# Pinning the involution's products in VectorE's order while keys and values are made

## The chip, the cores and the metric

The kernel runs on one core of one Trainium2 chip. The metric is device microseconds from the start to the end of one execution. All data are float32. The engines named below are PE (TensorE, with PEld for its weight loads), DVE (VectorE), ACT (ScalarE), POOL (GpSimd) and SP (SyncE, which only issues transfers here).

## The reference, cut to what matters

The input x has 4 images of 512 channels and 64 x 64 pixels. Layer 0 is self-attention over the 4096 pixels of an image with 128 inner channels. Layer 1 is a bottleneck block whose middle is an involution: a 7 x 7 convolution whose weights are made from the data, pixel by pixel.

```python
# layer 0, n = 4096 pixels of one image
q, k, v = wq @ x + bq, wk @ x + bk, wv @ x + bv            # 128 x n each
attn = softmax(q.T @ k, axis=-1)
x = wo @ (v @ attn.T) + bo + x                             # 512 x n
# layer 1
o1 = relu(s1 * (W1 @ x) + b1)                              # 128 x n
w = Ws @ relu(sr * (Wr @ o1) + br) + bs                    # 49 taps for each of 8 groups, per pixel
inv[c, pixel] = sum over 49 taps of w[group of c, tap, pixel] * o1[c, pixel moved by the tap]
out = s3 * (W3 @ inv) + b3 + x
```

## The kernel before, in words

**Stages.** The images b = 0 to 3 run one after the other. For each, `keys_values(b)` makes keys and values of 8 chunks of 512 pixels: four `pk` products (512 columns) and 16 `pv` products (128 columns) for each chunk. Then `attention(b)` goes through 8 blocks of 512 queries with 32 steps each: scores `pss` on PE, exponential `pt` on ACT, the product `po` with the values on PE, and the running sum `pacc` of the exponentials on DVE. After the last image a tail finishes what is left.

**Work woven in.** All that follows attention is cut into generators that are advanced by `chores()`, which is called four times for each chunk of `keys_values` and once for each step of `attention`. Three lists hold them:

- `finishing` (`finish_block`): what follows a block of queries. The row sums are inverted (`pl`, `rls`, `spread`), four `pwo` products are made, each of which DVE adds to x (L515), then the product `p1`, ACT's relu `o1` (L528), DVE's transpose `o1t` (L559), whose result eight transfers on SP write to `pix` in DRAM (L569), and `pr` and `red`, from which the tap weights come.
- `units`, worked off by `involution()` (L291 and on): a unit is four image rows. Its tap weights `pw` come from one step on PE. Then there are 14 (or 21) products: DVE multiplies image rows in a ring buffer by tap weights (L341), at first into `acc` and then into one of four `prod` buffers, and POOL adds each `prod` to `acc` (L365). Two last additions on POOL (L376) fold `acc`. The ring is loaded from `pix` by SP (`pump()`, L247). A product is called below by its place in its unit; product 0 is the one into `acc`.
- `closing` (`turn_unit`, `close_chunk`): transposes `pa` of a unit's `acc` on PE, ACT's copy to `accT` (L404), and, when two units make a chunk, four `py` products with W3, each of which DVE scales and adds to x (L419); then the store.

While keys and values of image b are made, the last pieces of image b-1 run beside them: the block finished last (chunk 7), chunk 5's `py`, the last products of unit 11, all of unit 12 and the first of unit 13. Image 0's stage has no earlier image beside it.

**PSUM.** `pl`, `spread`, `pwo`, `p1`, `pa`, `py`, `pr` and `pq` share the two buffers of the tag `mm`: a product into one of them waits for the reader of what was there before. `pw` has one buffer.

**What sets the order.** The Python code gives instructions in program order, with a model of the time of each engine: `pe` counts the time of PE's products, and `free` tells how long DVE, POOL and the DMA engines are booked. `involution()` gives no product while POOL is booked for longer than `lag` beyond `pe`. `lag` is `POOL_LAG[0]`, 4.0 us, in `keys_values`, and `POOL_LAG[1]`, 7.5 us, in `attention` and the tail:

```python
    for b in range(B):
        lag = POOL_LAG[0]
        kv = keys_values(b)
        lag = POOL_LAG[1]
```

The compiler then builds an instruction list for each engine. It follows program order as a priority, but by its own reckoning of times it takes an instruction that is ready before one that is not. So the order on an engine can differ from the program's. `tc.keep_in_program_order(ins)` gives the compiler an edge from the last instruction that the program gave to the same engine to `ins`: `ins` is not issued ahead of that one. It adds no wait at run time. The kernel before uses it in two other places (L282, L664).

Of the kernel before, what the change touches and what calls it, by code (L numbers as in the profile page):

```python
# [72 lines left out]
POOL_LAG = 4.0, 7.5  # L73
# [8 lines left out]
def fast_path(  # L82
# [20 lines left out]
    nc = tc.nc  # L103
# [51 lines left out]
    lag = 0.0  # L155
    low, load = 0, 0

    def until(us):
        while pe < us and not tail:
            yield "wait"  # L160
# [5 lines left out]
    def takes(engine, us):  # L166
        free[engine] = max(free[engine], pe) + us
        return free[engine]
# [39 lines left out]
    def mm(o, lhsT, rhs, start=True, stop=True, shared=1):  # L208
        pe_us(rhs.free_size() * PE_COLUMN / shared)
        return nc.tensor.matmul(o, lhsT=lhsT, rhs=rhs, start=start, stop=stop)  # L210
# [19 lines left out]
    def pump():  # L230

        nonlocal load
        while load // STEP in written:
            b, row = divmod(load, STEP)
            rows, us = written[b]

            end = H + SR - UR if rows == H else rows + PAD - 1
            n = min(b * STEP + end, low + RING) - load
            n = min(n, RING - load % RING, PIECE if b == B - 1 else RING)
            if n <= 0:  # L240
                break
            for h in range(2):
                src = pix[b % 2][row + h : row + h + n, :W, :]
                windows = bass.AP(
                    tensor=src.tensor, offset=src.offset, ap=[[P, W], [WP * P, n], [1, K * P]]
                )
                nc.sync.dma_start(  # L247
                    ring[h * W : (h + 1) * W, load % RING : load % RING + n]
                    .rearrange("p r x c -> p r (x c)"),
                    windows,  # L250
                )
            free["dma"] = max(free["dma"], us)
            us = takes("dma", ROW_US * n) + LAND_US
            landing.update((load + i, us) for i in range(n))
            load += n
            if row + n == H + SR - UR:
                load = (b + 1) * STEP
# [7 lines left out]
    def weights(b, u):  # L265
        red, col = reds[b, u]
        wpools.append(wpools.pop(0))
        pw = wpools[0].tile([P, NT, CH], F32, tag="w", name=f"pw_{b}_{u}")
        for t in range(NT):

            rows = slice(t * (P // NT), t * (P // NT) + CR + 1)
            pixels = slice(col, col + P)
            mm(
                pw[:, t, : NTAP * G], red[rows, pixels], wt[rows, O_WT : O_WT + NTAP * G],
                shared=2,
            )
        return pw


    def judge():  # L280
        ok = const.tile([P, B * N // TB], F32, name="ok")
        tc.keep_in_program_order(nc.vector.tensor_scalar(ok, rls, SAFE[0], None, ALU.is_ge))  # L282
        nc.vector.scalar_tensor_tensor(ok, rls, SAFE[1], ok, ALU.is_le, ALU.mult)
        okr = const.tile([P, 1], F32, name="okr")
        nc.vector.tensor_reduce(okr, ok, AX.X, ALU.min)
        pn = ps.tile([1, 1], F32, tag="mm", name="pn")
        nc.tensor.matmul(pn, lhsT=okr, rhs=ones[:, :1], start=True, stop=True)
        nc.vector.tensor_scalar(verdict, pn, P - 0.5, None, ALU.is_lt)


    def involution():  # L291
        nonlocal low, due
        while True:
            while not units:
                yield "none"
            b, u = units.pop(0)
            acc = work2.tile([P, NT, 4, P], F32, tag="acc", name=f"acc_{b}_{u}")
            yield from until(free["dve"] + 0.3)
            pw = early.pop((b, u), None) or weights(b, u)
            begin = pe + 0.5  # L300
            accp, ops = None, []
            base = b * STEP + u * UR
            for dy0, n in DYS:

                at = (base + dy0) % RING
                whole = at + n + NT < RING + 1
                pieces = [(dy0, n)] if whole else [(dy0, 2), (dy0 + 2, n - 2)]
                ops += [(x, dy, k) for x in range(K) for dy, k in pieces]
            for o, (x, dy, n) in enumerate(ops):
                if o and dy >= DYS[1][0] > ops[o - 1][1]:  # L310
                    low = base + UR
                    pump()
                    if tail and units:
                        early[units[0]] = weights(*units[0])
                rows = [(base + dy + t * 2) % RING for t in range(NT)]
                while base + dy + n + NT > load:
                    yield "wait"
                landed = max(landing[base + dy + i] for i in range(n + NT))
                while not tail and (
                    pe < max(begin, landed)  # L320
                    or free["dve"] > pe + (4.5 if b == B - 1 else 3.5)
                    or free["pool"] > pe + lag
                ):
                    yield "wait"
                free["pool"] = max(free["pool"], takes("dve", DVE_TAPS[0] + DVE_TAPS[1] * n))
                takes("pool", POOL_TAPS[0] + POOL_TAPS[1] * n)
                due -= n
                d0 = dy - DYS[dy >= DYS[1][0]][0]
                first = x == 0 and dy < DYS[1][0]
                prod, p0 = acc, d0  # L330
                if not first:
                    prod, p0 = prods.tile(
                        [P, NT, 4, P], F32, tag="prod", name=f"prod_{b}_{u}_{o}"
                    ), 0
                col = (x * K + dy) * G
                lines = ring[:, rows[0] : rows[0] + n, x, :]
                image = bass.AP(
                    tensor=lines.tensor, offset=lines.offset,
                    ap=[lines.ap[0], [(rows[1] - rows[0]) * K * P, NT], [K * P, n], [1, P]],
                )  # L340
                nc.vector.tensor_tensor(  # L341
                    prod[:, :, p0 : p0 + n, :].rearrange("p t d (g c) -> p t d g c", g=G),
                    image.rearrange("p t d (g c) -> p t d g c", g=G),
                    pw[:, :, col : col + n * G].unsqueeze(3)
                    .broadcast_to([P, NT, n * G, GC])
                    .rearrange("p t (d g) c -> p t d g c", d=n),
                    ALU.mult,
                )
                if first:
                    pass  # L350
                elif tail and o % 2 and (accp is not None or n > 1):

                    begin_sum = accp is None
                    if begin_sum:
                        accp = ps1.tile(
                            [P, NT, 2, P], F32, tag=("po", "acc")[u % 2], name=f"accp_{b}_{u}"
                        )
                    for d in range(0, n, 2):
                        k = min(2, n - d)
                        mm(  # L360
                            accp[:, :, :k, :], ident, prod[:, :, d : d + k, :],
                            begin_sum and d == 0, o + 2 >= len(ops) and d + 2 >= n,
                        )
                else:
                    nc.gpsimd.tensor_tensor(  # L365
                        acc[:, :, d0 : d0 + n, :], acc[:, :, d0 : d0 + n, :], prod[:, :, :n, :],
                        ALU.add,
                    )
                yield
            low = max(low, (b + 1) * STEP if u == NU - 1 else base + UR)  # L370
            pump()
            if (b, u) == (B - 1, NU - 1):
                judge()
            if accp is None:
                for n in (2, 1):
                    nc.gpsimd.tensor_tensor(  # L376
                        acc[:, :, :n, :], acc[:, :, :n, :], acc[:, :, n : 2 * n, :], ALU.add
                    )
            closing.append(turn_unit(b, u, acc, accp, takes("pool", POOL_OP * 1.5)))
# [217 lines left out]
    def attention(b, kt, vT):  # L597
# [22 lines left out]
        for m, (k, j) in enumerate(steps):  # L620
# [32 lines left out]
            chores()  # L653

    taps = [involution()]
# [4 lines that stand above are left out]
# [415 lines left out]
```

## Time and profile before

| | us |
|---|---|
| median of 3 runs | 2623.66 (2622.92 to 2625.16) |
| the profiled execution | 2624.13 |
| its span, first to last instruction | 2622.3 |
| PE busy | 2599.3 (99%) |
| DVE busy | 1865.5 (71%) |
| POOL busy | 1821.0 (69%) |
| ACT busy | 857.2 (33%) |

The stages in the span are: keys and values of image 0 until about 62 us; of image 1 from 617 to 695; of image 2 from 1256 to 1332; of image 3 from 1893 to 1970; attention between them; the tail from about 2540. Times in the timelines are us from the start of the span. A line of a timeline gives start and duration, then engine, line of the code, operation, output and inputs with their shapes, how many instructions were merged (x2 for one product of float32, which takes two passes), and in brackets the engine's idle time just before and who ended it.

### The profile page before, as it was taken

How to read it: one execution, taken by the hardware profiler on the slowest of the kernel's cores; microseconds unless marked ns; L12 is line 12 of the kernel's file. 1: busy time of each engine (PE TensorE's matmuls, PEld its weight loads, DVE VectorE, ACT ScalarE, POOL GpSimd, SP SyncE). 2: the span in 40 equal slices, each digit the busy share in tenths (PEclk: the TensorE clock that was granted, in tenths of full speed). 3: DMA queues.
4: the chain of work that ended last, by engine and by line, in shares of the span. 5: the costliest groups of instructions: out<-in, count | busy, mean ns of one | idle time of the engine just before them, and what ended most of it. 6: DMA issues, size and time to landing. Idle time of an engine off the chain costs nothing.

```text
span 2622.3 us, 24098 instructions
## 1 busy us (share of the span) xinstructions
PE 2599.3 (99%) x7382; PEld 1242.0 (47%) x7382; DVE 1865.5 (71%) x2626; ACT 857.2 (33%) x1430; POOL 1821.0 (69%) x1197
## 2 busy tenths in 40 slices
PE   9999999999999999999999999999999999999998
PEld 7444444445544444444554444444464444444574
DVE  0347887877575787888576677878757768787887
ACT  1333333332233333333223333333313333333330
POOL 0007887878781787888875467888787667777876
PEclk9999999999999999999999999999999999999999
DMA  6032323336514244322541433434453423222343
GB/s 235 0 74 60 75 64 75 69 89 156 139 40 106 60 93 92 87 71 61 153 116 36 103 61 92 93 92 93 92 154 88 107 60 89 68 61 60 77 91 101
DMA packets 143898, 231.70 MB, mean 88 GB/s; under 512 B 57032, under 2 KB 63632, under 8 KB 143632
## 3 DMA queue, kind: packets, MB, share of 16 engines
q1 hardware_dynamic: 143328, 229.71, 36.2%
q8 instruction: 60, 0.98, 0.2%
q14 instruction: 78, 0.64, 0.1%
q10 hardware_dynamic: 432, 0.36, 0.0%
HBM read 187.28 MB, written 42.77 MB: 88 GB/s over the span
## 4 chain that ended last, share of the span: by engine, by line
PE 94%; POOL 3%; DVE 2%; DMA 0%; issue 0%; ACT 0%; POOLq 0%; DVEq 0%; ACTq 0%
PE pss L210 34%; PE po L210 33%; PE pq L210 4%; PE pwo L210 4%; PE p L210 4%; PE py L210 4%; PE pv L210 4%; PE pk L210 3%; POOL acc L365 3%; PE pw L210 2%; DVE prod L341 1%; PE pr L210 1%; PE pa L393 0%; PE accp L210 0%; DVE x L419 0%
## 5 line engine op out<-in xcount | busy, mean ns | idle before, releaser
L365 POOL TENSOR_TENSOR acc<-acc,prod 128x768 f32<-128x768 f32 (+3 forms) x1063 | 1699.0, 1616 | 777.0 <-DVE prod L341 726.2
L210 PE MATMUL pss<-q,k 128*128 128x512 f32 (+1 forms) x2112 | 1055.0, 584 | 2.3 <-ACT q L471 2.3
L210 PE MATMUL po<-pt,v 128*128 128x512 f32 (+1 forms) x2112 | 1047.5, 580 | 0.0
L615 ACT ACTIVATE pt<-pss 128x512 f32<-128x512 f32 x1024 | 611.5, 597 | 1225.6 <-PE pss L210 1201.7
L341 DVE TENSOR_TENSOR prod<-ring,pw 128x512 f32<-128x512 f32 (+3 forms) x1092 | 902.1, 850 | 100.7 <-POOL acc L365 87.7
L646 DVE TENSOR_TENSOR pacc<-pacc,pt 128x512 f32<-128x512 f32 x958 | 666.2, 695 | 379.7 <-ACT pt L615 372.9
L210 PEld LDWEIGHTS po<-pt,v 128*128 128x128 f32 x2112 | 399.3, 190 | 480.3 <-issue 460.2
L210 PEld LDWEIGHTS pss<-q,k 128*128 128x128 f32 x2112 | 389.6, 190 | 452.3 <-issue 432.6
L210 PE MATMUL py<-accT,wt 128*128 128x512 f32 (+1 forms) x264 | 132.8, 586 | 7.8 <-DVE x L419 6.7
L210 PE MATMUL pwo<-on,wt 128*128 128x512 f32 (+1 forms) x264 | 129.3, 583 | 0.0
L210 PEld LDWEIGHTS pv<-wt,x 128*128 128x128 f32 x1024 | 121.7, 195 | 15.8 <-issue 15.6
L515 DVE SCALAR_TENSOR_TENSOR x<-pwo,bo,x 128x512 f32<-128x512 f32 (+1 forms) x132 | 96.3, 734 | 45.5 <-PE pwo L210 44.0
L376 POOL TENSOR_TENSOR acc<-acc 128x512 f32<-128x512 f32 x120 | 119.5, 996 | 9.4
L210 PE MATMUL pv<-wt,x 128*128 128x128 f32 x1024 | 123.3, 279 | 0.0
L341 DVE TENSOR_TENSOR acc<-ring,pw 128x1024 f32<-128x1024 f32 (+1 forms) x84 | 79.4, 964 | 61.1 <-PE pw L210 58.9
L533 ACT ACTIVATE x<-x,vec 128x512 f32<-128x512 f32 (+1 forms) x132 | 92.8, 706 | 81.5 <-PE p L210 76.4
L210 PE MATMUL p<-x,wt 128*128 128x512 f32 (+1 forms) x264 | 119.2, 579 | 0.0
L210 PE MATMUL pk<-x,wt 128*128 128x512 f32 x256 | 117.1, 597 | 0.3 <-DMA x<-x_dram 0.3
L419 DVE SCALAR_TENSOR_TENSOR x<-py,vec,x 128x512 f32<-128x512 f32 (+1 forms) x132 | 95.9, 726 | 29.8 <-PE py L210 28.1
L210 PE MATMUL pq<-x,wt 128*128 128x512 f32 (+1 forms) x264 | 115.5, 580 | 0.0
L210 PEld LDWEIGHTS py<-accT,wt 128*128 128x128 f32 x264 | 49.3, 191 | 65.3 <-issue 48.5
L210 PEld LDWEIGHTS pq<-x,wt 128*128 128x128 f32 x264 | 49.8, 190 | 58.7 <-issue 56.4
(58 smaller groups left out, 723.0 us busy)
## 6 DMA issues: line engine op xcount, KB each, us to landing
x<-x_dram SPq DMA_DIRECT2D x55, 1024.0 KB, 6.0
ring<-pix SPq DMA_DIRECT2D x74, 448.0 KB, 10.9
ring<-pix SPq DMA_DIRECT2D x24, 1344.0 KB, 18.3
out_dram<-x SPq DMA_DIRECT2D x31, 1024.0 KB, 4.4
ring<-pix SPq DMA_DIRECT2D x24, 896.0 KB, 14.0
ring<-pix SPq DMA_DIRECT2D x30, 672.0 KB, 11.2
ring<-pix SPq DMA_DIRECT2D x6, 2240.0 KB, 19.1
pix<-o1t SPq DMA_DIRECT2D x192, 32.0 KB, 1.7
```

The lines of the kernel that those rows point to most:

```text
L210: return nc.tensor.matmul(o, lhsT=lhsT, rhs=rhs, start=start, stop=stop)
L341: nc.vector.tensor_tensor(prod[:, :, p0 : p0 + n, :].rearrange("p t d (g c) -> p t d g c", g=G), image.rearrange("p t d (g c) -> p t d g c ...
L365: nc.gpsimd.tensor_tensor(acc[:, :, d0 : d0 + n, :], acc[:, :, d0 : d0 + n, :], prod[:, :, :n, :], ALU.add,)
L376: nc.gpsimd.tensor_tensor(acc[:, :, :n, :], acc[:, :, :n, :], acc[:, :, n : 2 * n, :], ALU.add)
L419: nc.vector.scalar_tensor_tensor(xt[:, t, :], py, v1(V_S3 + t), xt[:, t, :], ALU.mult, ALU.add)
L515: nc.vector.scalar_tensor_tensor(xt[:, t, :], pw, bo[:, t : t + 1], xt[:, t, :], ALU.add, ALU.add)
L533: nc.scalar.activation(xt[:, t, :], xt[:, t, :], AF.Identity, bias=v1(V_B3 + t))
L615: nc.scalar.activation(pt, pss, AF.Exp)
L646: nc.vector.tensor_tensor(paccs[k], paccs[k], pt, ALU.add)
```

## The change

The product that DVE makes is kept in a variable, and while `lag` is that of `keys_values`, the product is pinned behind the instruction that the program gave to DVE before it. Products given in attention or in the tail are not pinned, nor is any other instruction.

```diff
-                nc.vector.tensor_tensor(
+                product = nc.vector.tensor_tensor(
                     prod[:, :, p0 : p0 + n, :].rearrange("p t d (g c) -> p t d g c", g=G),
                     image.rearrange("p t d (g c) -> p t d g c", g=G),
                     pw[:, :, col : col + n * G].unsqueeze(3)
...
                     ALU.mult,
                 )
+                if lag == POOL_LAG[0]:
+                    tc.keep_in_program_order(product)
                 if first:
                     pass
```

## The prediction

> **What bounds the kernel now.** I read the engines' busy time first, then the busy time by stage, then what TensorE waited for, then the timelines of one stage. The page and the stages (columns: stretch, its length, busy us and instructions of PE, PEld, DVE, ACT, POOL, then clock, DMA share, GB/s):
>
> ```profile
> PE 2599.3 (99%) x7382; PEld 1242.0 (47%) x7382; DVE 1865.5 (71%) x2626; ACT 857.2 (33%) x1430; POOL 1821.0 (69%) x1197
> ...
> 630.00:715.00 85.00, 81.80 (x349) 48.47 (x350) 44.29 (x57) 20.75 (x34) 66.81 (x43) 0.98 0.55 144
> 715.00:1262.00 547.00, 547.00 (x1363) 240.86 (x1362) 417.07 (x593) 189.86 (x316) 395.49 (x259) 1.00 0.35 80
> 1262.00:1345.00 83.00, 80.09 (x369) 49.20 (x368) 46.66 (x59) 19.63 (x32) 71.51 (x45) 1.00 0.62 164
> ...
> 1893.00:1980.00 87.00, 84.06 (x391) 53.24 (x390) 46.76 (x58) 19.72 (x32) 68.96 (x42) 0.98 0.66 170
> ...
> 2540.00:2623.00 83.00, 70.19 (x268) 40.67 (x266) 66.38 (x94) 7.49 (x17) 54.21 (x34) 0.96 0.36 93
> ```
>
> TensorE has no idle time in attention (547.00 of 547.00), so only a stage where it idles can shorten the run: the three stages that make keys and values while an earlier image's involution is finished (about 3 us idle each), and the tail (13 us). The change acts in the first three. There the waits of PE name one cause, three times:
>
> ```profile
> PE py L210 <- DVE x L419: 6.7, 3, 2.4
> ```
>
> The timelines of PE, VectorE and GpSimd around the first of the three (start, duration, what, idle before it and who ended it):
>
> ```profile
> 652.47 1.02 PE L210 MATMUL py<-accT,wt 128*128 128x512 f32 x2
> ...
> 656.76 1.88 PE L210 MATMUL pk<-x,wt 128*128 128x512 f32 x4
> 661.06 2.03 PE L210 MATMUL py<-accT,wt 128*128 128x512 f32 x2 [2.42 <-DVE x L419]
> 662.89 4.54 PE L210 MATMUL pv<-wt,x 128*128 128x128 f32 x32
> ```
> ```profile
> 655.61 0.95 DVE L341 TENSOR_TENSOR prod<-ring,pw 128x768 f32<-128x768 f32 x1 [1.47 <-POOL acc L365]
> 657.51 0.95 DVE L341 TENSOR_TENSOR prod<-ring,pw 128x768 f32<-128x768 f32 x1 [0.94 <-POOL acc L365]
> 659.39 0.96 DVE L341 TENSOR_TENSOR prod<-ring,pw 128x768 f32<-128x768 f32 x1 [0.93 <-POOL acc L365]
> 660.26 0.74 DVE L419 SCALAR_TENSOR_TENSOR x<-py,vec,x 128x512 f32<-128x512 f32 x1
> ...
> 662.15 0.70 DVE L559 STREAM_TRANSPOSE o1t<-o 128x512 f32<-128x512 f32 x1
> ```
> ```profile
> 641.03 27.77 POOL L365 TENSOR_TENSOR acc<-acc,prod 128x1024 f32<-128x1024 f32 x13 [2.19 <-DVE prod L341]
> 668.88 2.07 POOL L376 TENSOR_TENSOR acc<-acc 128x512 f32<-128x512 f32 x2
> 679.47 21.61 POOL L365 TENSOR_TENSOR acc<-acc,prod 128x1024 f32<-128x1024 f32 x13 [8.53 <-DVE prod L341]
> ```
>
> The second py product of the chunk ends at 653.5. The addition that reads it (L419) runs only at 660.26, behind products of unit 12 that each wait for one of four prod buffers, which GpSimd frees. In the program, products 5 to 12 of the unit come after this addition (the numbering in the compiled instruction list shows it); they stand ahead of it because the compiler, which orders each engine's list by readiness in its own reckoning, moved them. The third py product needs that addition's PSUM buffer, so GpSimd's pace reaches TensorE.
>
> [...] the addition's input was ready for 6.7 us and it did not pass a waiting product. [...] clock 0.72 over 661.06 to 667.26 after 2.42 us, the same 0.72 over 1936.66 to 1942.82 after 2.16 us, and 1.00 after the 2.13 us at 1299.68. So the drop is a part of the price of the wait, not a certain one.
>
> **The change part by part.** No instruction, DMA or semaphore wait is added: the call gives the compiler an ordering edge to the VectorE instruction before the product in the program. What moves is the order on VectorE while the lag is 4.0, so in the three stages (the first stage, 0 to 62 us, has no unit to work on). I laid out the first with durations of the rows above: DVE product 1.15 us (1024 columns) or 0.88 (768), addition and transpose 0.68, POOL addition 2.375 or 1.865, and 1.06 us from the start of a PE product to its reader.
>
> *What goes away.* With the py1 addition at 653.5 to 654.2, the third py product starts when PE is free, at 658.48, and not at 661.06: 2.58 us. It then takes 0.86 and not 1.83 us (0.97), and the next 32 pv products 3.57 and not 4.37 (0.80): 4.35 us in this stage. The second has 2.29 of start and 0.10 of py (2.39), the third 2.32, 0.10 and 1.63 of pv (4.05). **Sum 10.8 us**, of which 7.2 are waiting and 3.6 a slow clock. After taking these out, the time from the pw product of unit 12 to the transposes pa of unit 12 is 42.35 us in all three, which says that nothing else differs between them.
>
> *What is late next: products, then POOL.* In program order, the products queue behind additions that wait for PE. Unit 11's last three wait for the pwo additions at 630.44 and 634.81: POOL idles 1.8 us and ends the unit at 640.5, not 638.9. Its transposes come on PE at 642.67: covered. In unit 12, product 2 waits for pwo3 (642.87; POOL idle 1.8), product 5 for py1 (653.53; 3.5), product 6 for the transpose o1t behind ScalarE's o (657.74; 1.8). With 0.2 before product 1 that is 7.3 us idle where before had 2.2 us, and all of it ahead. POOL ends the unit at 677.3 by this working, which gives 670.1 for the old order where the trace has 670.95; so 677.3 to 678.1. Who waits: unit 13's first POOL addition, which before started at 679.47, and which now has its product at 674.9 (pw of unit 13 comes on PE at 671.65). So the 8.53 us of POOL idle cover the loss. The transposes of unit 12 now come on PE at 679.6: **slack 1.5 to 2.3 us**. The pw product needs product 13 read, at 668.6: slack 3 us.
>
> *Other queues.* The transpose moves from 662.15 to about 657.7; the eight pix writes behind it on SP (issued from 662.88), the x load among them that waits for PE's pv, the store and the six ring loads from 674.0 move forward by about 4 us with PE, so the wait of 3.53 us for the ring at 690.97 keeps its place relative to PE. Only ScalarE's o feeds the transpose; its order is as before. POOL enters attention 2 to 3 us later relative to PE. The exponentials have five pt buffers, and in this trace ScalarE there waits for PE's scores alone; the next pw product came on PE at 714.75 while POOL had ended at 709.65, 5 us of slack that absorb it. I take 0 for this, with 0 to 1 us per stage as its bounds. The wait of 0.78 us for q at the start of attention stays.
>
> *Not shown.* Compiling anew can also alter choices in the last image's attention and the tail, where PE idles 13 us: I take 0, with -2 to +2 us.
>
> **Sum**: the profiled execution took 2624.13 us (span 2622.3 and 1.8 around it), 0.5 above the median 2623.66. 2624.1 - 10.8 = 2613.3; from the median, 2612.9. I say **2613**.
>
> **Rivals.**
> *A smaller gain: another wait takes the place.* With two mm buffers in PSUM, py2 may get the one that ScalarE's o releases (657.74), and py3 the one of py2's addition (660.2); PE needs them at 658.48 and 662.9. Margins of 0.7 and 2.7 us speak against it. If such a wait of 1 to 2 us per stage appears, with or without the slow clock, the gain is 3 to 8 us: 2616 to 2621.
> *No change.* A new wait of 2.4 us in each stage gives all of it back: 2622 to 2625. That the edges do nothing is excluded by the order in the timelines, save that the additions could be held by something that I do not see; what speaks against is that PE's second py product had ended 6.7 us earlier.
> *Slower: GpSimd becomes the bound at unit 12's transposes.* Products pinned behind PE starve POOL; when it ends the unit d after 679.6, PE waits d at pa in each stage. 3 d has to pass 10.8 us before the kernel loses, and 16 us before it shows: d over 5.3, so 7 us more POOL idle than the 7.3 worked out, about twice as much. With d = 6: 2613 + 18 = 2631. For it: POOL is 90% busy in 638 to 671. Against: 8.5 us of idle follow.
>
> **Numbers.** Differences within 0.2% (5.2 us) count as none. The full gain (2610 to 2616) 0.72; smaller gain 0.12, most of it over 5.2 us; none 0.10; slower 0.06. So faster 0.81, same 0.13, slower 0.06. The range runs from 2609.5 (full gain and 3 us of luck in the tail) to 2619, which takes in the waits without the clock part (2616.5) and part of the smaller gains.
>
> **What would show it.** Right: the wait of PE py for DVE x near zero (from 6.7 us); DVE L419 within 1.2 us of its py product; o1t about 4 us earlier; no clock below 0.95 in the three stages; POOL idle before unit 13 under 1 us, and gaps of 2 to 4 us inside unit 12. Wrong: PE waiting for POOL at pa, or for ScalarE's o at py, or attention stages with PE idle.

## The result and the profile after

The changed kernel took **2614.22 us** in the median of 6 runs (2612.28 to 2614.82), the kernel before 2623.77 (2622.92 to 2625.76) beside it: a ratio of 0.9959, 95% interval 0.9949 to 0.997. The profiled execution had a span of 2610.5 us, 11.8 less than before. In the two profiles PE, ScalarE, GpSimd and SP each run their instructions in the same order. VectorE's order differs in three places, one in each stage that makes keys and values beside an earlier image.

The page's busy time, and the busy time by stage (columns as in the prediction; the stages now end earlier, so the stretches do too):

```profile
PE 2594.3 (99%) x7382; PEld 1237.5 (47%) x7382; DVE 1863.7 (71%) x2626; ACT 856.8 (33%) x1430; POOL 1821.7 (70%) x1197
...
630.00:711.00 81.00, 80.22 (x346) 46.97 (x345) 46.71 (x60) 20.75 (x34) 65.81 (x43) 1.00 0.57 151
711.00:1258.00 547.00, 547.00 (x1369) 241.42 (x1368) 417.13 (x593) 190.10 (x317) 396.42 (x260) 1.00 0.35 80
1258.00:1339.00 81.00, 80.22 (x362) 48.77 (x361) 45.90 (x59) 19.90 (x33) 70.44 (x45) 1.00 0.62 165
...
1884.00:1968.00 84.00, 83.22 (x394) 52.24 (x393) 44.53 (x55) 19.71 (x32) 67.59 (x41) 1.00 0.70 178
...
2528.00:2611.00 83.00, 70.12 (x268) 40.49 (x266) 66.28 (x94) 7.42 (x17) 54.12 (x34) 0.96 0.36 93
```

PE's idle time in the three stages fell from about 3 us each to 0.78, and the clock there is 1.00. Attention (547.00 of 547.00) and the tail are as they were. What PE waited for, the upper part of the list:

```profile
PE accp L210 <- DVE prod L341: 2.4, 1, 2.4
PE pss L210 <- ACT q L473: 2.3, 3, 0.8
PE pa L210 <- POOL acc L367: 1.9, 1, 1.9
```

The 6.7 us of py waiting for DVE x have left the list, and nothing took their place. The first stage on PE, VectorE and GpSimd:

```profile
655.53 1.88 PE L210 MATMUL pk<-x,wt 128*128 128x512 f32 x4
657.25 1.02 PE L210 MATMUL py<-accT,wt 128*128 128x512 f32 x2
658.11 3.73 PE L210 MATMUL pv<-wt,x 128*128 128x128 f32 x32
```
```profile
652.30 0.75 DVE L421 SCALAR_TENSOR_TENSOR x<-py,vec,x 128x512 f32<-128x512 f32 x1 [4.27 <-PE py L210]
652.97 1.21 DVE L341 TENSOR_TENSOR prod<-ring,pw 128x1024 f32<-128x1024 f32 x1
656.54 0.71 DVE L561 STREAM_TRANSPOSE o1t<-o 128x512 f32<-128x512 f32 x1 [2.37 <-ACT o L530]
```
```profile
643.66 7.22 POOL L367 TENSOR_TENSOR acc<-acc,prod 128x1024 f32<-128x1024 f32 x3 [1.51 <-DVE prod L341]
654.32 2.35 POOL L367 TENSOR_TENSOR acc<-acc,prod 128x1024 f32<-128x1024 f32 x1 [3.44 <-DVE prod L341]
658.50 15.60 POOL L367 TENSOR_TENSOR acc<-acc,prod 128x1024 f32<-128x1024 f32 x8 [1.83 <-DVE prod L341]
674.18 2.08 POOL L378 TENSOR_TENSOR acc<-acc 128x512 f32<-128x512 f32 x2
676.22 19.70 POOL L367 TENSOR_TENSOR acc<-acc,prod 128x1024 f32<-128x1024 f32 x11
```

The second py addition now starts 1.06 us after its product, VectorE stands idle ahead of it (4.27 us) instead of PE behind it, and the third py product follows pk without a gap. GpSimd pays inside unit 12 (1.51, 3.44 and 1.83 us of idle time) and gets it back ahead of unit 13, where its 8.53 us of idle time are gone.

A measure that the start of the span doesn't disturb is the time on PE from the pw product of unit 12 to the transposes pa of unit 12. It is used below for all kernels (pw to pa, in us):

| kernel | stage 1 | stage 2 | stage 3 | pa of stage 3 to the end |
|---|---|---|---|---|
| before | 46.70 | 44.74 | 46.40 | 662.8 |
| after | 42.34 | 42.34 | 42.34 | 663.0 |

The three stages give 10.8 us. Another 1.2 us of the 11.8 in the span come from the first 62 us, where no product is pinned and where PE reached pb at 60.67 instead of 61.89; over all profiles here the pw product of stage 1 comes between 636.04 and 637.55, so this start moves by 1.5 us. It is not part of the gain.

### The profile page after: what moved, and what is told of

It is laid out like the page before. It is cut to its first block, busy times and chain, and to the rows that moved or that the text cites. A ratio compares the mean times of both kernels' runs of the same rounds, so it can differ in the third digit from the quotient of the medians.

```text
span 2610.5 us, 24098 instructions
## 1 busy us (share of the span) xinstructions
PE 2594.3 (99%) x7382; PEld 1237.5 (47%) x7382; DVE 1863.7 (71%) x2626; ACT 856.8 (33%) x1430; POOL 1821.7 (70%) x1197
## 4 chain that ended last, share of the span: by engine, by line
PE 97%; DVE 1%; POOL 1%; issue 0%; ACT 0%; POOLq 0%; DVEq 0%; ACTq 0%
PE pss L210 34%; PE po L210 33%; PE pv L210 4%; PE pk L210 4%; PE pwo L210 4%; PE pq L210 4%; PE p L210 4%; PE py L210 4%; PE pw L210 2%; POOL acc L367 1%; DVE prod L341 1%; PE pr L210 1%; PE pa L395 1%; PE accp L210 0%; DVE x L421 0%
## 5 line engine op out<-in xcount | busy, mean ns | idle before, releaser
L210 PEld LDWEIGHTS p<-x,wt 128*128 128x128 f32 x264 | 49.9, 190 | 58.3 <-issue 54.1
```

## The experiments

Times are medians, the ratio is to the kernel before on the same chip, whose median was 2625.3 to 2625.4 us in these sessions.

**The changed kernel again** (`again`, no edit).

> The changed kernel once more, for the price of the wait and its spread. Theory W (all of the gain is TensorE's wait at the third py product, 7.2 us in three stages, and the slow clock that follows some of these waits, 0 to 3.6 us): 8 to 12 us under the kernel before, no PE wait of py for DVE x, and no stretch with a clock under 0.95 in the stages of keys and values. If the slow clock had nothing to do with the wait (rival C), it would be seen here again at the same places, and the gain would be 7 us.

Measured: 2613.98 us (5 runs), ratio 0.9958 (0.9944 to 0.9971). PE has no wait of py for DVE x, all three stages have clock 1.00, and pw to pa is 42.34 us three times. Theory W holds; rival C has nothing to show.

**Only the late part of unit 12** (`late12`).

```diff
-                if lag == POOL_LAG[0]:
+                if lag == POOL_LAG[0] and u == 12 and o >= 5:
```

> Only the products of unit 12 from product 5 on are pinned; those of units 11 and 13 and products 1 to 4 are free as before. VectorE's list then has the second py addition two places behind the first and ahead of product 5, as in the changed kernel; the four pwo additions stay late. Theory W: the whole gain, 2612 to 2615 us, PE wait of py near 0. Rival P (the earlier pwo additions, or the whole order, bring a part): visibly less, 2617 or more.

Measured: 2613.83 us, ratio 0.9958 (0.9944 to 0.9971), pw to pa 42.34 us three times. Nine pins in each stage are enough; rival P falls.

**All but that part** (`rest`).

```diff
-                if lag == POOL_LAG[0]:
+                if lag == POOL_LAG[0] and not (u == 12 and o >= 5):
```

> The complement: all products of the three stages are pinned except those of unit 12 from product 5 on. The compiled list has the second py addition behind product 9 and not behind product 12, and the transpose o1t still behind product 12. Product 9 waits for POOL's addition of product 5, which by the working of the prediction ends near 654.3 us of the first stage; so the addition runs at about 655.2 to 655.9, ahead of the 658.48 at which PE wants the buffer. Theory W: the whole gain as well, 2612 to 2615, although o1t stays at about 661 to 662 and the products run ahead of most additions. Rival O (the gain comes from the earlier transpose, pix writes and ring loads): little or no gain, 2620 or more.

Measured: 2614.08 us, ratio 0.9959 (0.9945 to 0.9973), pw to pa 42.34 us three times. VectorE in the first stage:

```profile
653.91 0.95 DVE L341 TENSOR_TENSOR prod<-ring,pw 128x768 f32<-128x768 f32 x1 [1.36 <-POOL acc L367]
654.78 0.74 DVE L421 SCALAR_TENSOR_TENSOR x<-py,vec,x 128x512 f32<-128x512 f32 x1
...
661.02 0.70 DVE L561 STREAM_TRANSPOSE o1t<-o 128x512 f32<-128x512 f32 x1
```

The second py addition is still behind a product that waits for GpSimd, but behind product 9: it ends at 655.5, before PE wants the buffer at 657.78. The transpose is as late as in the kernel before, and the gain is whole. So neither strict program order nor the earlier transpose matters, only whether this one addition ends in time. Rival O falls.

**The third py product later, nothing pinned** (`later_py`, on the kernel before).

```diff
-            for _ in range(2):
+            for _ in range(4 if t == 1 and lag == POOL_LAG[0] else 2):
                 yield
```

> Nothing is pinned. In the stages of keys and values close_chunk lets two more steps pass between the second and the third py product, so that PE makes the 16 pv products of the chunk (3.57 us) in between. VectorE's list stays as before: the second py addition is still behind product 12 and runs at about 660.3, the transpose at about 662. PE then asks for the buffer at about 662.05, after the addition has ended at 661.0. Theory W: PE's wait is gone although VectorE's order is the old one, and so is the time: 2612 to 2616. Rival O (VectorE's order itself, o1t and what follows from it): no gain, 2621 to 2625.

Measured: 2613.26 us, ratio 0.9957 (0.9943 to 0.9971); pw to pa 42.34 us three times. PE, and VectorE, in the first stage:

```profile
658.01 3.73 PE L210 MATMUL pv<-wt,x 128*128 128x128 f32 x32
661.58 1.02 PE L210 MATMUL py<-accT,wt 128*128 128x512 f32 x2
```
```profile
658.92 0.95 DVE L341 TENSOR_TENSOR prod<-ring,pw 128x768 f32<-128x768 f32 x1 [0.94 <-POOL acc L365]
659.79 0.74 DVE L419 SCALAR_TENSOR_TENSOR x<-py,vec,x 128x512 f32<-128x512 f32 x1
```

The addition is as late as ever, behind product 12. PE simply has something else to do until it ends. In the three stages VectorE's order is that of the kernel before; only two products of unit 13 come later, in attention, where PE has no idle time. The same gain with the old order in the stages shows that the lost time was PE's wait and what followed it there, and not VectorE's order as such. Rival O falls here too.

**Three and five prod buffers, unpinned** (`p3`, `p5`, on the kernel before).

```diff
-    prods = pool("prods", 4)
+    prods = pool("prods", 3)        # p5: 5
```

> The kernel before with three prod buffers instead of four; VectorE's list is the same in the three stages. Theory W: the second py addition is behind product 12, and with three buffers product 12 waits for POOL's addition of product 9 instead of 8, one POOL addition (1.87 us) later. PE's wait at the third py product grows from about 2.2 to about 4.1 us in each stage, 6.7 to about 12.3 in all; time 5.6 us more than before, or up to 9 with slow clock: 2629 to 2635. Rival B (the wait is not set by POOL through the prod buffers, but by a position alone): 6.7 us as before, 2622 to 2626.

> The kernel before with five prod buffers; same list in the three stages, nothing pinned. Theory W: product 12 waits for POOL's addition of product 7, 1.87 us earlier, so the addition ends at about 659.1 where PE wants the buffer at 658.48: PE waits 0.3 to 0.7 us per stage, 1 to 2 us in all instead of 6.7. Gain 5 us of waiting and up to 3.6 of slow clock: 2615 to 2619. Rival B: as before, 2622 to 2626.

Measured: 2646.77 us with three, ratio 1.0085 (1.0071 to 1.0099), and 2612.47 us with five, ratio 0.9954 (0.994 to 0.9967). PE's third py product of the first stage, with three and then with five buffers:

```profile
662.16 2.08 PE L210 MATMUL py<-accT,wt 128*128 128x512 f32 x2 [4.32 <-DVE x L419]
664.03 5.16 PE L210 MATMUL pv<-wt,x 128*128 128x128 f32 x32
```
```profile
658.40 1.13 PE L210 MATMUL py<-accT,wt 128*128 128x512 f32 x2 [0.52 <-DVE x L419]
659.37 3.73 PE L210 MATMUL pv<-wt,x 128*128 128x128 f32 x32
```

The wait is 4.32, 2.42 and 0.52 us with 3, 4 and 5 buffers: 1.9 us for each, which is about one addition of GpSimd (1.81 us) and the step to the next. That is how GpSimd's pace reached PE, and rival B falls. In the other two stages five buffers leave waits of 0.25 and 0.26 us. pw to pa is 49.26, 48.24 and 49.22 with three, 43.13, 42.86 and 42.87 with five. In the three stages the expectations hold: three buffers cost 8.9 us there and five save 9.0. The totals were missed, by about 12 us with three and by 2.5 us with five, because the buffers also count where I had not looked: from pa of stage 3 to the end, three buffers cost 13.7 us and five save 1.9.

**Three buffers, pinned** (`p3_pin`, the changed kernel with the same edit).

> The changed kernel with three prod buffers. Theory W: with the additions ahead of the products, PE does not meet POOL's pace, so the number of buffers has no price in the three stages: PE wait of py near 0, 2612 to 2616, that is 15 us under the kernel before with three buffers. Rival (products pinned behind PE need the fourth buffer, and POOL falls so far behind that PE waits at the transposes pa of unit 12): PE wait of pa for POOL of several us, 2617 or more.

Measured: 2627.26 us, ratio 1.0009 (1.0001 to 1.0018). In the three stages the expectation holds: pw to pa 42.34 us three times, so with the products pinned the loss of the fourth buffer costs nothing there. The total was missed by 11 us. The time from pa of stage 3 to the end is 675.1 us where the changed kernel has 663.0, and PE's new waits are there and not at pa of unit 12: those of py for rls in the attention of the last image, those of accp in the tail. Of the 12.1 us, 3.9 are lost by the last po product and 8.2 after it.

```profile
PE accp L210 <- DVE prod L341: 6.3, 5, 3.2
PE py L210 <- DVE rls L503: 2.5, 2, 1.7
```

Against `p3`, pinning is worth 19.5 us, of which the three stages have 19.7 (6.92, 5.90, 6.88).

**The kernel before again** (`before_again`, no edit).

> The kernel before once more, with another profile, for the share of the slow clock. Theory W with the clock as a part of the wait's price: PE again waits 2.1 to 2.6 us at the third py product in three stages, and a slow stretch follows some of these waits and no place where PE did not wait; the time from pw to pa of unit 12 is 44.6 to 46.8 us where the changed kernel has 42.3. Rival C (the slow clock comes at its own times): slow stretches at other places or before the wait.

Measured: 2625.41 us, ratio 1.0002 (0.9994 to 1.001). The same three waits, 6.7 us in all; pw to pa 46.70, 44.77 and 46.39. Stages 2 and 3 on PE:

```profile
1299.01 1.12 PE L210 MATMUL py<-accT,wt 128*128 128x512 f32 x2 [2.16 <-DVE x L419]
1299.97 3.73 PE L210 MATMUL pv<-wt,x 128*128 128x128 f32 x32
```
```profile
1935.97 1.12 PE L210 MATMUL py<-accT,wt 128*128 128x512 f32 x2 [2.15 <-DVE x L419]
1936.94 5.36 PE L210 MATMUL pv<-wt,x 128*128 128x128 f32 x32
```

Waits of the same length, and a slow stretch after that of stage 3 only: its 32 pv products took 5.36 us where those of stage 2 took 3.73. The mean clock of the three stages was 0.98, 1.00 and 0.98, the same in this profile as in the first, and attention had 1.00. After the waits of 4.0 us and more in `p3` the stages had 0.96, 0.98 and 0.96, after those of 0.25 to 0.52 us in `p5` 1.00 three times. Rival C falls: in these stages the clock was slow only in profiles where PE had waited there.

**Pinned everywhere but in the tail** (`everywhere`).

```diff
-                if lag == POOL_LAG[0]:
+                if not tail:
```

> As the changed kernel, with the products pinned in attention too, and only in the tail not. PE has no idle time in attention, so theory W expects no further gain: 42.3 us from pw to pa of unit 12 as in the changed kernel, 2612 to 2616 in all. Rival G (GpSimd, fed later by products that queue behind additions, becomes the bound, or the last image's list and the tail turn out worse): 2617 or more, with PE waiting for POOL or for DVE in attention.

Measured: 2614.29 us, ratio 0.9959 (0.9945 to 0.9972); pw to pa 42.34 us three times. VectorE's order in attention changes at many places, and the time does not, since PE waits for none of it there. Rival G did not come, though PE's longest wait in the tail grew from 2.4 to 3.3 us.

**The first query product earlier** (`q_early`, on the changed kernel; `attention` gets q0 and starts with it).

```diff
                 kt[:, c * CH : (c + 1) * CH], pk, AF.Identity, bias=v1(V_BK)
             )
+            if i == NCH - 1:
+                q0 = queries(b, 0, 0, CH)
             pv = ps1.tile([P, 4, P], F32, tag=("po", "acc")[i % 2], name=f"pv_{b}_{c}")
```

> The changed kernel, and the first query product pq of an image is made ahead of the last chunk's pv products instead of after them, so that ScalarE's q (0.69 us) is done while PE makes pv. Takes away the wait of 0.78 us that PE has in three images (2.3 us in all) at the first score. Expected: that wait at 0, 2 to 3 us less than the changed kernel, 2611 to 2612.5, if the second mm buffer is free at that time; if pq then waits for the reader of the transposes pa, nothing is gained or up to 1 us lost per image.

Measured: 2610.47 us, ratio 0.9946 (0.9932 to 0.996), 3.5 us under `again`, a little more than expected. The wait of pss for ACT q is gone from PE's list; from one image's pw of unit 12 to the next image's is 633.50 us and was 634.55.

**Five buffers, pinned, and all three together** (`p5_pin` and `best`).

> The changed kernel with five prod buffers. The stages of keys and values have no wait left that a buffer could shorten: 42.3 us as in the changed kernel, where the kernel before with five buffers has 42.9 to 43.1. In the tail five buffers alone seem to bring 1 to 2 us (the kernel before with five buffers took 2612.5 although its three stages are 1.8 us longer than those of the changed kernel). So 2610 to 2612.5, 1 to 2.5 under the kernel before with five buffers.

> Pinned products, five prod buffers, and the first query product ahead of the last pv products. The three gains act at different places (the wait at py, the tail, the wait for q), so they should add: about 2 us under the changed kernel with five buffers, 2607.5 to 2610.5. If five buffers change the tail's list for the worse with the other program order, 2610 to 2613.

Measured: 2611.45 us, ratio 0.9948 (0.9934 to 0.9961), and **2608.24 us, ratio 0.9934 (0.9921 to 0.9948)**. With five buffers pw to pa is 42.34 us pinned; `best` is 5.7 us under `again`, and the two single steps are 2.5 and 3.5. They add within 0.3 us, as places that do not touch each other should. `best` is the fastest kernel here.

## Why the prediction was right

- *The place and the mechanism*: PE's third py product waited for an addition that stood behind products paced by GpSimd. `later_py` (PE's side moved), `rest` (the addition moved part of the way) and the row of 3, 4 and 5 buffers show each link of it.
- *The size*: 7.2 us of waiting and 3.6 us of slow clock, 10.8 in all; the three stages gave 4.36, 2.40 and 4.06, 10.8 in all. The medians gave 9.6 us at first and 11.3 in `again`. The difference lies within the spread of executions, of which the first 62 us have 1.5.
- *Counting the slow clock as part of the wait's price* was a choice, and it held: without it the forecast would have been 2616.5. Its 3.6 us were read from one profile; `before_again` has the same.
- *What is late next*: worked out for GpSimd in unit 12 were 7.3 us of idle time (0.2, 1.8, 3.5, 1.8), found 7.3 (0.50, 1.51, 3.44, 1.83). That the sum fits so exactly is luck: two parts are 0.3 us off, in opposite directions. The end of the unit was put at 677.3 to 678.1; it came at 676.26, which is 677.5 when the start's 1.2 us are added. The slack at the transposes was put at 1.5 to 2.3 us and was 2.1 (676.26 to 678.38). The slower rival needed 5.3 us past that slack and stayed far off.
- *The order of queues*: the transpose o1t was put at about 657.7 and came at 656.54 in a span that starts 1.2 us earlier. The wait for the ring, which was to keep its place relative to PE, is hidden now behind GpSimd's later additions (1.75 us at 685.92, put down to POOL). This was a small miss without a price.
- *Bounds taken and not needed*: nothing changed in attention or the tail. No instruction changed places there; only the three places differ.
- *The rival "another wait takes the place"* did not come: ScalarE's o released its buffer in time.

## What to carry to other kernels

When an engine that bounds the kernel waits for a buffer, look at where the buffer's reader stands in its own queue: a short instruction that is ready (here for 6.7 us) can stand behind long-waiting ones of another chain, and the wait then has that chain's pace (here 1.9 us for each buffer). Such a link is cut by the reader's place or by giving the waiting engine other work first (both brought all of the 10.8 us here), and nearly so by one more buffer in the chain ahead of it (9.0 us); choose the one that costs nothing elsewhere. And price a wait of the bounding engine with what follows it, here half as much again in slow clock (3.6 us on 7.2), and check what the delayed engine's next idle time can absorb before trusting the gain.

## What the runs showed of the hardware that was not expected

Of six waits of only 2.13 to 2.43 us (`before` and `before_again`), four came with a slow clock, always in the same two of three stages (mean clock of the stage 0.98, in the spared one 1.00); the three waits of 4.0 to 4.3 us in `p3` all did (0.96 to 0.98); of the three of 0.25 to 0.52 us in `p5` none did (1.00). So waits of about one length did not have one price here: in the kernel before, that of stage 2 cost 2.40 us from pw to pa and that of stage 3 cost 4.06.

The kernel before, cut at the ends of the waits of stages 2 and 3, shows each wait and what ran behind it (after the stretch come its length, then PE's busy time; the clock is the third number from the end):

```profile
1297.39:1299.68 2.29, 0.16 (x1) 0.00 (x1) 1.62 (x2) 0.69 (x1) 2.21 (x2) 1.00 0.00 0
1299.68:1304.21 4.53, 4.53 (x34) 4.05 (x35) 2.21 (x3) 0.00 (x0) 4.29 (x4) 1.00 0.20 33
1934.34:1936.66 2.32, 0.16 (x1) 0.00 (x0) 1.62 (x2) 0.69 (x1) 2.24 (x2) 1.00 0.00 0
1936.66:1942.82 6.16, 6.16 (x34) 5.68 (x35) 2.21 (x3) 0.00 (x0) 5.85 (x5) 0.72 0.21 35
```

The mean of 0.72, on which the prediction rested, hides a clock of 0.50 over a part of the stretch and of 1.00 over the rest: 0.50 from 661.14 to 664.55 in stage 1 and from 1937.73 to 1941.14 in stage 3.

Why stage 2 was spared is not shown. The length of the wait does not tell it: 2.13 us in stage 2 and 2.16 in stage 3 in `before`, 2.16 and 2.15 in `before_again`. These figures are no threshold for other work.

The end of the run, from pa of stage 3 on, proved far more sensitive to prod buffers than the stages studied: 12 to 14 us lost for the fourth buffer and 2 us won by a fifth. A few instructions of VectorE also change places in the tail in these kernels; how much is due to that and how much to the buffers was not separated.
